# A router's top logit taken tile by tile, and a head's sums moved to GpSimd, in a four-layer graph network on one core

## The chip, the core and the metric

The kernel runs on one NeuronCore of a Trainium2 chip. The core has five engines that run their own instruction streams side by side: TensorE (PE, matrix products into PSUM), VectorE (DVE), ScalarE (ACT), GpSimd (POOL) and SyncE (SP, which here only issues transfers). Each engine takes its instructions in order; semaphores order them against each other. The metric is the device time of one execution in microseconds (us); less is better.

## The reference, cut to what matters

A network of four layers on 1250 nodes with 512 features and 20000 edges. Each layer is a graph step and a feed-forward step, each added to x after a layer norm. The change touches two of the eight steps: the mixture of experts of layer 1 and the first of two attention convolutions of layer 2.

```python
def _L1_ffn_ref(x, Wr, br, W1, b1, W2, b2):        # 8 experts, top 1
    xf = x.reshape(-1, d)
    router_logits = xf @ Wr + br
    topk_logits, topk_idx = jax.lax.top_k(router_logits, 1)
    topk_gates = jax.nn.softmax(topk_logits, axis=1)
    for e in range(8):
        h = relu(xf @ W1[e] + b1[e])
        oe = h @ W2[e] + b2[e]
        out = out + where((topk_idx[:, 0] == e)[:, None], topk_gates * oe, 0.0)

def gat_conv(x, src, dst, W, att_src, att_dst, bias):   # 4 heads of 256
    h = (x @ W).reshape(N, HEADS, HID)
    a_src = sum(h * att_src, axis=-1)
    a_dst = sum(h * att_dst, axis=-1)
    e = leaky_relu(a_src[src] + a_dst[dst], 0.2)
    m = segment_max(e, dst, num_segments=N)
    e = exp(e - m[dst])
    s = segment_sum(e, dst, num_segments=N)
    alpha = e / (s[dst] + 1e-16)
    out = segment_sum(alpha[:, :, None] * h[src], dst, num_segments=N)
    return out.reshape(N, HEADS * HID) + bias
```

With one expert per node the gate is softmax of one number, which is 1; only the index of the largest logit is needed.

## The kernel before

The nodes stand in NT = 10 tiles of P = 125 rows; x stays in SBUF as X. The program is written stage after stage, and a framework schedules the instructions onto the engines, puts in the semaphores and gives out buffers: a tile of a pool or a PSUM bank that one engine writes and another reads brings a wait. It sees dependences by tile, so that two engines that touch different columns of one PSUM tile wait for each other.

**Routing of layer 1.** `l1_route` hands a function `done(i)` to the stage before it (the end of layer 1's graph step, batch normalisation of ten tiles), which calls it as each tile of X is ready. For every pair of tiles, `done` forms the layer norm: statistics on VectorE (`bn_stats`, L2186), a square root on ScalarE (L2193), six small VectorE steps that end in `nmr` (L2194 to L2199), the scaling on ScalarE (`f1n_xn`, L2212), transposes on PE (L2246) and their copy out of PSUM on ScalarE (`f1n_t`, L2253). `later(i, xt)` multiplies the transposed tile with the router's weights (L814): four products that fill 8 columns of one PSUM tile, `f.logits[0]`, which holds the logits of all ten tiles side by side.

`l1_ffn` then sorts the nodes by expert. It adds the bias to all logits at once (L858), takes the maximum and its index for each tile (L863, L864), and makes a mask `mk` of chosen experts (L868). Two products on PE count nodes before each node (L872) and in each tile (L874). From the counts VectorE makes, for each expert, the number of groups of 128 rows (`gn`) and the last group's end (`gend`); from `gend` it derives whether more than 13 groups are in use (`more`) and each group's expert (`eg`, `es`, `ei`, L891 to L899); then each node's place in the sorted order (`inc`, `pos`, `posi`, L900 to L910). Places become one-hot matrices (`sl`, `gr`, L913 to L924), a product turns them into node numbers by group (L927), and `node` (L929) is the list by which GpSimd gathers rows (`fetched`). SP reads `ei` and loads that expert's weights `f1w` and biases `f1b`. PE then transposes the gathered rows (L944) and runs `up` (L953) and `down` for 13 groups.

**First convolution of layer 2.** `gat` is called twice; the first has `kt = 4`, and there `late` is true. It works on weights between all source and destination nodes: a step (h, s) is head h and source tile s, and an array `e` of 125 x 1250. For each step VectorE forms the exponent (`exponents`, L1125), ScalarE takes the exponential (L1126), VectorE multiplies with the number of edges (`counted`, L1131), PE multiplies `e` with the nodes' features into six accumulators (`aggregated`, L1141), and VectorE adds `e` to `sums` (`summed`, L1150), from which the softmax's denominator comes. There are four heads of ten steps. Step n's loop body issues exponents of step n + 2, counts of n + 1, the sum and the products of n. In the first convolution `maxima(2, ...)` for heads 2 and 3 is spread over the first five steps: two maxima of 125 x 1250 (L1068) for each tile, with its mask `g_mb` loaded by GpSimd's queue (L1066). After it `turned(2)` puts their result through PE (L1087). At the end of a head ScalarE copies the accumulators out (`evacuated`, L1155), and in the first step of the next head `rows_out` sums `sums` over its rows on PE (L1164). Tiles `e` come from a pool of seven buffers, so an exponent waits until the readers of the buffer's last tile are done.

Of the kernel before, what the change touches and what calls it, by code (L numbers as in the profile page):

```python
# [9 lines left out]
F32 = mybir.dt.float32  # L10
F16 = mybir.dt.float16
BF16 = mybir.dt.bfloat16
I32 = mybir.dt.int32
U32 = mybir.dt.uint32
U16 = mybir.dt.uint16
AF = mybir.ActivationFunctionType
OP = mybir.AluOpType
AX = mybir.AxisListType
# [5 lines left out]
P = 125  # L24
NT = N // P
# [11 lines left out]
class Net:  # L37
# [760 lines left out]
    def l1_route(self, ctx):  # L798

        nc, a, X, ne = self.nc, self.a, self.X, 8  # L800
        f = self.f1 = SimpleNamespace()
        p = f.p = self.pool(ctx, "f1")
        f.xnd = self.tc.dram_tile([N, D], F32, name="f1xn")
        f.norm = Norm(self, ctx, "f1n", keep="rows", scalar=True)
        f.wr = p.tile([128, 4, ne], F32, name="f1wr")
        nc.gpsimd.dma_start(f.wr, a["L1_ffn_Wr"].rearrange("(k p) e -> p k e", p=128))
        f.br = self.rowbc(p, a["L1_ffn_br"], ne, "f1br")
        f.logits = {}

        def later(i, xt):  # L810
            if not f.logits:
                f.logits[0] = self.bank("f1_ps")
            for k in range(4):
                nc.tensor.matmul(f.logits[0][:P, i * ne:(i + 1) * ne], lhsT=xt[:, k, :],  # L814
                                 rhs=f.wr[:, k, :], start=k == 0, stop=k == 3)

        xts = {}

        def done(i):
            if not f.norm.pair(i, X):  # L820
                return
            for j in (i - 1, i):
                nc.gpsimd.dma_start(f.xnd[j * P:(j + 1) * P, :], f.norm.xn[:, j, :])
                xts[j] = f.norm.turned(j)
            for j in (i - 3, i - 2):
                if j >= 0:
                    later(j, xts.pop(j))
            if i == NT - 1:
                for j in (i - 1, i):
                    later(j, xts.pop(j))  # L830

        return done

    def l1_ffn(self, done):
        nc, tc, a, X = self.nc, self.tc, self.a, self.X
        ne, hid, ng, nm = 8, 256, 17, 13
        ys = tc.dram_tile([ng * 128, D], F32, name="f1ys")
        with ExitStack() as ctx:
            p, xnd = self.f1.p, self.f1.xnd
# [7 lines left out]
            for t in range(NT):  # L847
# [6 lines left out]

            lg = p.tile([P, NT, ne], F32, name="f1lg")
            nc.vector.tensor_tensor(lg, self.f1.logits[0][:P, :NT * ne].rearrange("p (t e) -> p t e", t=NT),  # L858
                                    self.f1.br[:P, None, :].to_broadcast([P, NT, ne]), OP.add)
            m8 = p.tile([P, NT, 8], F32, name="f1m8")  # L860
            i8 = p.tile([P, NT, 8], U32, name="f1i8")
            for i in range(NT):
                nc.vector.max(m8[:, i, :], lg[:, i, :])  # L863
                nc.vector.max_index(i8[:, i, :], m8[:, i, :], lg[:, i, :])  # L864
            i1 = p.tile([P, NT], F32, name="f1i1")
            nc.vector.tensor_copy(i1, i8[:, :, 0])
            mk = p.tile([P, ne, NT], F32, name="f1mk")
            nc.vector.tensor_tensor(mk, i1[:, None, :].to_broadcast([P, ne, NT]),  # L868
                                    self.iota[:P, :ne, None].to_broadcast([P, ne, NT]), OP.is_equal)
# [7 lines left out]
            inc = p.tile([P, ne, NT], F32, name="f1inc")  # L877
# [8 lines left out]
            gn = p.tile([P, ne], F32, name="f1gn")  # L886
            nc.vector.tensor_copy(gn, gi)
            gend = p.tile([P, ne], F32, name="f1gend")
            nc.vector.tensor_tensor_scan(gend, self.ones[:P, :ne], gn, 0.0, OP.mult, OP.add)
            more = p.tile([1, 1], I32, name="f1more")  # L890
            nc.vector.tensor_scalar(more, gend[0:1, ne - 1:], float(nm), -float(nm), OP.max, OP.add)  # L891
            eg = p.tile([1, ng, ne], F32, name="f1eg")
            nc.vector.tensor_tensor(eg, self.iota[0:1, :ng, None].to_broadcast([1, ng, ne]),
                                    gend[0:1, None, :].to_broadcast([1, ng, ne]), OP.is_ge)
            es = p.tile([1, ng], F32, name="f1es")
            nc.vector.tensor_reduce(es, eg, AX.X, OP.add)
            nc.vector.tensor_scalar(es, es, float(ne - 1), None, OP.min)
            ei = p.tile([1, ng], I32, name="f1ei")
            nc.vector.tensor_copy(ei, es)  # L899
            nc.vector.tensor_tensor(gend, gend, gn, OP.subtract)  # L900
            nc.vector.tensor_tensor(inc, inc, tot, OP.subtract)
            nc.vector.scalar_tensor_tensor(inc, gend[:, :, None].to_broadcast([P, ne, NT]), 128.0, inc,
                                           OP.mult, OP.add)
            nc.vector.tensor_tensor(inc.rearrange("p e t -> p (e t)"), inc.rearrange("p e t -> p (e t)"),
                                    ps[:P, :ne * NT], OP.add)
# [2 lines left out]
            nc.vector.tensor_reduce(pos, inc.rearrange("p e t -> p t e"), AX.X, OP.add)  # L908
            posi = p.tile([P, NT], I32, name="f1posi")
            nc.vector.tensor_copy(posi, pos)  # L910

            qi = p.tile([P, 2, NT], I32, name="f1qi")
            nc.vector.tensor_scalar(qi[:, 0], posi, 127, None, OP.bitwise_and)  # L913
# [16 lines left out]
            xg, xt, w, b, h = {}, {}, {}, {}, {}  # L930
# [78 lines left out]
    def gat(self, HT, H, kt, wa, W, bias, name):  # L1009

        nc, tc = self.nc, self.tc
# [5 lines left out]
        with ExitStack() as ctx:  # L1017
            p = self.pool(ctx, name)
# [14 lines left out]
            def wide(rows, what):  # L1033
                return qt.tile([rows, N], F32, name=name + what, tag="t")
# [11 lines left out]
            for h in range(nh):  # L1046
                t = wide(128, "_asb")
# [53 lines left out]
            qb, es, accs, first = {}, {}, {}, {}  # L1101
# [14 lines left out]
            late = kt == 4  # L1116
# [3 lines left out]
            sums = p.tile([P, N], F32, name=name + "_sum")  # L1120
# [25 lines left out]
                    first[h] = e  # L1146

            def summed(h, s):
                if s > 0:
                    nc.vector.tensor_tensor(sums, sums if s > 1 else first.pop(h), es[h, s], OP.add)  # L1150

            def evacuated(h):
                for f in range(2):
# [62 lines left out]
            for n, (h, s) in enumerate(steps):  # L1216
                if late and n < 5:
                    maxima(2, range(2 * n, 2 * n + 2))
                if n == 5:
                    turned(2)  # L1220
                if s == 1 and h + 1 < nh:
                    terms(h + 1)
                if n + 2 < len(steps):
                    exponents(*steps[n + 2])
                if n + 1 < len(steps):
                    counted(*steps[n + 1])
                summed(h, s)
                aggregated(h, s)
                if s == 3 and h > 0:
                    reciprocals(h - 1)  # L1230
                if s == 7 and h > 0:
                    divided(h - 1)
                if s == NT - 1 and h + 1 < nh:
                    evacuated(h)
# [1154 lines left out]
```

## Time and profile before

| What | Value |
|---|---|
| Median of 3 runs | 2718.39 us (2718.12 to 2720.2) |
| The profiled execution | 2713.25 us |
| Its span, first to last instruction | 2711.5 us |
| Mean granted TensorE clock | 0.929 |
| VectorE, exponent L1125, 125x1250 | 1517 ns each, x80 |
| VectorE, count L1131, 125x1250 | 1453 ns each, x80 |
| VectorE, sum L1150, 125x1250 | 1456 ns each, x64 (and 1461 ns, x8) |
| VectorE, maximum L1068, 125x1250 | 1460 ns each, x80 |
| ScalarE, exponential L1126, 125x1250 | 1335 ns each, x80 |
| PE, products L1141 | 519 ns each, x960 |
| PE, logits L814 | 355 ns each, x80 (two records for one product) |

The counts are those of both convolutions together. The profile lists one execution: a busy share for each engine over the span, the chain of work that ended last, groups of instructions by line, and a timeline in which each row is a start, a length, an engine with a line, the operation and its tiles. In brackets stands the idle time of that engine just before, and what ended it. Lengths of rows that follow each other on one engine overlap a little: the end of one lies under the start of the next.

### The profile page before, as it was taken

Reading aid. Unit: us, or ns where it says so; the run is one execution under the profiler, and the core shown is the slowest. Engines: PE = TensorE matmul, PEld = TensorE weight load, DVE = VectorE, ACT = ScalarE, POOL = GpSimd, SP = SyncE. Lnnn points to the kernel's source line nnn. Section 1 sums busy time; section 2 is a strip of 40 time slices with the busy share of each in tenths; the row PEclk is TensorE's granted clock in tenths of the full one; section 3 lists DMA queues with packets and bytes.
Section 4 is the critical chain, followed back from the end, with each engine's and each line's share of the span. In section 5 each row is a group of like instructions: output and inputs, shape, how many; then the busy total and the mean of one; then the engine's idle time right before and its main releaser. Section 6 shows DMA issues by size and latency. Waiting matters only on the chain.

```text
span 2711.5 us, 29770 instructions
## 1 busy us (share of the span) xinstructions
PE 2430.8 (90%) x10367; PEld 1538.4 (57%) x10367; DVE 1415.8 (52%) x3219; ACT 820.3 (30%) x1824; POOL 475.8 (18%) x540
## 2 busy tenths in 40 slices
PE   6899889999996999885879899999999799869996
PEld 3555689999943767764534454445554344445542
DVE  8856562100054888864257995567953653621100
ACT  4541111212123777752122342023421231211110
POOL 0002111211004555511210000100010121122211
PEclk9999769999986999995979999999999899979998
DMA  3112245666605555512832102211122201469996
GB/s 84 51 36 77 70 139 188 213 207 204 199 28 143 149 147 142 143 36 93 333 116 85 60 16 92 83 52 45 44 69 93 86 2 49 155 240 361 365 377 239
DMA packets 106746, 360.03 MB, mean 133 GB/s; under 512 B 34818, under 2 KB 39703, under 8 KB 84828
## 3 DMA queue, kind: packets, MB, share of 16 engines
q1 hardware_dynamic: 59867, 252.68, 26.4%
q0 software_dynamic: 44560, 100.92, 14.1%
q10 hardware_dynamic: 2160, 4.45, 0.5%
q8 instruction: 84, 1.38, 0.2%
q14 instruction: 75, 0.61, 0.1%
HBM read 328.36 MB, written 29.53 MB: 132 GB/s over the span
## 4 chain that ended last, share of the span: by engine, by line
PE 40%; DMA 8%; DVE 6%; issue 2%; ACT 1%; POOL 0%; POOLq 0%; ACTq 0%; SPq 0%; DVEq 0%
PE g_acc L1141 11%; PE g_ps L1097 7%; DMA f3wd<-in_L_ffn_W_down_dram 4%; PE f_ps L1616 3%; PE g_ps L1277 3%; PE f_ps L1590 2%; PE g_ps L1486 2%; PE g_ps L1459 1%; PE g_ps L1464 1%; PE f_ps L1340 1%; DMA f1ys<-f1y 1%; DVE g_junk L1068 1%; PE g_ps L1040 1%; PE ac_ps L1814 1%; DMA CT<-in_L_ffn_W_down_dram 1%
## 5 line engine op out<-in xcount | busy, mean ns | idle before, releaser
L1141 PE MATMUL g_acc<-g_e,g2hh 125*128 125x417 f32 (+1 forms) x960 | 344.6, 519 | 7.4 <-DVE g_e L1131 7.4
L1141 PEld LDWEIGHTS g_acc<-g_e,g2hh 125*128 125x128 f32 x960 | 182.9, 192 | 166.8 <-issue 157.3
L428 POOL DMA_INDIRECT G<-t,SI x160 | 156.4, 978 | 231.7 <-issue 104.2
L1804 ACT ACTIVATE G<-G,ex 128x129 f32<-128x129 f32 x632 | 190.1, 389 | 0.8
L1814 PE MATMUL ac_ps<-G,oh 128*125 128x258 f32 x736 | 187.3, 410 | 1.8 <-DVE g1acc L1823 1.5
L564 PE MATMUL f_ps<-f0xgt,f0w 128*128 128x187 f32 x1024 | 168.8, 325 | 0.1
L1814 PEld LDWEIGHTS ac_ps<-G,oh 128*125 128x125 f32 x736 | 143.5, 200 | 42.3 <-issue 11.9
L575 PE MATMUL f_acc<-f0ht,f0w 128*128 128x187 f32 x1024 | 166.7, 324 | 0.0
L564 PEld LDWEIGHTS f_ps<-f0xgt,f0w 128*128 128x128 f32 x1024 | 165.5, 192 | 0.4 <-DVE f0xgt L105 0.3
L575 PEld LDWEIGHTS f_acc<-f0ht,f0w 128*128 128x128 f32 x1024 | 164.7, 191 | 0.3
L1125 DVE SCALAR_TENSOR_TENSOR g_e<-g_qb,g_a 125x1250 f32<-125x1250 f32 x80 | 120.6, 1517 | 69.3 <-DMA g_qb<-g_qd 61.7
L1126 ACT ACTIVATE g_e<-g_e,g_a 125x1250 f32<-125x1250 f32 x80 | 106.4, 1335 | 137.6 <-DVE g_e L1125 137.3
L1616 PE MATMUL f_ps<-f3wd,f3ht 128*39 128x512 f32 (+1 forms) x544 | 134.6, 613 | 14.2 <-DMA f3wd<-in_L_ffn_W_down_dram 14.1
L1622 DVE TENSOR_SCALAR f3y<-f_ps,f3k_wsel 39x512 f32<-39x512 f32 x32 | 24.0, 749 | 230.7 <-PE f_ps L1616 230.2
L1097 PE MATMUL g_ps<-g22w,g2ht 128*125 128x512 f32 x320 | 138.0, 593 | 0.1
L224 PE MATMUL c_ps<-ohs,ohd 128*125 128x512 f16 (+1 forms) x552 | 108.1, 344 | 22.5 <-DVE ohd L215 13.3
L1068 DVE CUSTOM_DVE_ANT_0 g_junk<-g_mb,g_asb 125x1250 f32<-125x1250 bf16 x80 | 116.8, 1460 | 19.5 <-DMA g_asb<-g_as 15.0
L1131 DVE SCALAR_TENSOR_TENSOR g_e<-g_e,CT 125x1250 f32<-125x1250 f32 x80 | 116.0, 1453 | 7.0 <-ACT g_e L1126 6.7
L1765 DVE TENSOR_REDUCE gm<-mx_ps 125x1 f32<-125x512 f32 x184 | 114.0, 682 | 3.7 <-PE mx_ps L1756 3.7
L592 DVE TENSOR_SCALAR f0y<-f_ps,f0xg,f0r 128x512 f32<-128x512 f32 (+1 forms) x16 | 12.2, 802 | 187.2 <-PE f_ps L590 187.2
L218 DVE TENSOR_SCALAR ohs<-iota,ES 128x1250 f16<-128x1250 f16 x184 | 89.2, 542 | 34.5 <-PE c_ps L224 31.7
L224 PEld LDWEIGHTS <-ohd 128*125 128x125 f16 x552 | 69.0, 137 | 62.3 <-DVE ohd L215 14.0
(678 smaller groups left out, 3862.2 us busy)
## 6 DMA issues: line engine op xcount, KB each, us to landing
f0w<-in_L_ffn_w_dram SPq DMA_DIRECT2D x64, 1024.0 KB
f3wd<-in_L_ffn_W_down_dram SPq DMA_DIRECT2D x48, 1280.0 KB
CT<-in_L_ffn_W_down_dram SPq DMA_DIRECT2D x16, 1280.0 KB
f1w<-in_L_ffn_w_dram SPq DMA_DIRECT2D x13, 1024.0 KB
f3wu<-in_L_ffn_W_up_dram SPq DMA_DIRECT2D x12, 1024.0 KB
g_mb<-mbd POOLq DMA_DIRECT2D x40, 305.2 KB, 3.4
g_qb<-g_qd SPq DMA_DIRECT2D x16, 625.0 KB
f2tv<-in_L_ffn_tv_W_dram SPq DMA_DIRECT2D x16, 512.0 KB
```

The source lines that it names most:

```text
L224: nc.tensor.matmul(pss[i][:P, :cn], lhsT=ohd[g % 2][:, k, :], rhs=ohs[(4 * g + k) % R][:, c0:c0 + cn], start=g == 0 and k == 0, stop=k == ...
L428: self.nc.gpsimd.indirect_dma_start(out=out, out_offset=None, in_=table, in_offset=bass.IndirectOffsetOnAxis(ap=idx, axis=0))
L564: nc.tensor.matmul(ps[:, :cap], lhsT=w[:, k, f * 128:(f + 1) * 128], rhs=xgt[e][:, k, :], start=k == 0, stop=k == 3)
L575: nc.tensor.matmul(acc[e][d][:, :cap], lhsT=w[:, f, d * 128:(d + 1) * 128], rhs=ht[e][:, 4 * c + f, :], start=c == 0 and f == 0, stop=c == ...
L1068: nc.vector.tensor_tensor_reduce(junk, mb, asb[h], 1.0, -3e38, OP.add, OP.max, accum_out=mx[:, i, h:h + 1])
L1097: nc.tensor.matmul(ps[:P, :], lhsT=HT[:, k, i * P:(i + 1) * P], rhs=ws[hf][k // 4][:, k % 4, :], start=k == 0, stop=k == kt - 1)
L1125: nc.vector.scalar_tensor_tensor(e, qb[h][0], A8[:, s, h:h + 1], qb[h][1], OP.add, OP.max)
L1131: nc.vector.scalar_tensor_tensor(e, e, 1.0, self.CT[:, s, :], OP.min, OP.mult)
L1141: nc.tensor.matmul(accs[h][f][c][:, :cn], lhsT=H[:, s, h * 256 + f * 128:h * 256 + (f + 1) * 128], rhs=e[:, c0:c0 + cn], start=s == 0, sto ...
L1616: nc.tensor.matmul(ps[64 * h:64 * h + k, :], lhsT=ht[g][:n, f, j * k:(j + 1) * k], rhs=ws[h][:n, f - f0, :], start=f == 0, stop=f == nf - 1)
L1804: nc.scalar.activation(gv[:, k, h], gv[:, k, h], AF.Copy, scale=ex[:, k, h:h + 1])
L1814: nc.tensor.matmul(ac[j][:P, 0:2 * (ch + 1)], lhsT=v["oh"][:, k, :], rhs=v["G"][:, k, j * 2 * (ch + 1):(j + 1) * 2 * (ch + 1)], start=k == ...
```

## The change

There are three parts.

(a) `later` adds the bias to its tile's eight logits and takes their maximum and index itself, right after the tile's products; `l1_ffn` no longer does so for all tiles.

(b) In `l1_ffn` the steps for `more`, `eg`, `es` and `ei` move behind `posi`. Two copies of one element of `posi` into `more` and `eg` are new; they make these steps depend on `posi`, so that they can't be scheduled before it. The groups' start goes to a tile of its own, `gof`, since `gend` is still needed.

(c) In `summed`, the nine additions of head 0 in the first convolution are issued on GpSimd instead of VectorE.

```diff
         def later(i, xt):
...
             for k in range(4):
                 nc.tensor.matmul(f.logits[0][:P, i * ne:(i + 1) * ne], lhsT=xt[:, k, :],
                                  rhs=f.wr[:, k, :], start=k == 0, stop=k == 3)
+            nc.vector.tensor_tensor(f.lg[:, i, :], f.logits[0][:P, i * ne:(i + 1) * ne], f.br[:P, :], OP.add)
+            nc.vector.max(f.m8[:, i, :], f.lg[:, i, :])
+            nc.vector.max_index(f.i8[:, i, :], f.m8[:, i, :], f.lg[:, i, :])
...
-            lg = p.tile([P, NT, ne], F32, name="f1lg")
-            nc.vector.tensor_tensor(lg, self.f1.logits[0][:P, :NT * ne].rearrange("p (t e) -> p t e", t=NT),
-                                    self.f1.br[:P, None, :].to_broadcast([P, NT, ne]), OP.add)
-            m8 = p.tile([P, NT, 8], F32, name="f1m8")
-            i8 = p.tile([P, NT, 8], U32, name="f1i8")
-            for i in range(NT):
-                nc.vector.max(m8[:, i, :], lg[:, i, :])
-                nc.vector.max_index(i8[:, i, :], m8[:, i, :], lg[:, i, :])
             i1 = p.tile([P, NT], F32, name="f1i1")
-            nc.vector.tensor_copy(i1, i8[:, :, 0])
+            nc.vector.tensor_copy(i1, self.f1.i8[:, :, 0])
...
-            more = p.tile([1, 1], I32, name="f1more")
-            nc.vector.tensor_scalar(more, gend[0:1, ne - 1:], float(nm), -float(nm), OP.max, OP.add)
-            eg = p.tile([1, ng, ne], F32, name="f1eg")
...
-            nc.vector.tensor_copy(ei, es)
-            nc.vector.tensor_tensor(gend, gend, gn, OP.subtract)
+            gof = p.tile([P, ne], F32, name="f1gof")
+            nc.vector.tensor_tensor(gof, gend, gn, OP.subtract)
...
             nc.vector.tensor_copy(posi, pos)
+
+            more = p.tile([1, 1], I32, name="f1more")
+            nc.vector.tensor_copy(more, posi[0:1, 0:1])
+            nc.vector.tensor_scalar(more, gend[0:1, ne - 1:], float(nm), -float(nm), OP.max, OP.add)
+            eg = p.tile([1, ng, ne], F32, name="f1eg")
+            nc.vector.tensor_copy(eg[0:1, 0, 0:1], posi[0:1, 0:1])
+            nc.vector.tensor_tensor(eg, self.iota[0:1, :ng, None].to_broadcast([1, ng, ne]),
+                                    gend[0:1, None, :].to_broadcast([1, ng, ne]), OP.is_ge)
+            es = p.tile([1, ng], F32, name="f1es")
+            nc.vector.tensor_reduce(es, eg, AX.X, OP.add)
+            nc.vector.tensor_scalar(es, es, float(ne - 1), None, OP.min)
+            ei = p.tile([1, ng], I32, name="f1ei")
+            nc.vector.tensor_copy(ei, es)
...
             def summed(h, s):
+
+                eng = nc.gpsimd if late and h == 0 else nc.vector
                 if s > 0:
-                    nc.vector.tensor_tensor(sums, sums if s > 1 else first.pop(h), es[h, s], OP.add)
+                    eng.tensor_tensor(sums, sums if s > 1 else first.pop(h), es[h, s], OP.add)
```

More of the change, by code (lines that the diff above doesn't have):

```diff
@@ L808, in l1_route @@
         f.logits = {}
+        f.lg = p.tile([P, NT, ne], F32, name="f1lg")
+        f.m8 = p.tile([P, NT, 8], F32, name="f1m8")
+        f.i8 = p.tile([P, NT, 8], U32, name="f1i8")
         def later(i, xt):
@@ L889, in l1_ffn @@
             nc.vector.tensor_tensor_scan(gend, self.ones[:P, :ne], gn, 0.0, OP.mult, OP.add)
-            more = p.tile([1, 1], I32, name="f1more")
-            nc.vector.tensor_scalar(more, gend[0:1, ne - 1:], float(nm), -float(nm), OP.max, OP.add)
-            eg = p.tile([1, ng, ne], F32, name="f1eg")
[L893 to L898, printed above, removed]
-            nc.vector.tensor_copy(ei, es)
-            nc.vector.tensor_tensor(gend, gend, gn, OP.subtract)
+            gof = p.tile([P, ne], F32, name="f1gof")
+            nc.vector.tensor_tensor(gof, gend, gn, OP.subtract)
             nc.vector.tensor_tensor(inc, inc, tot, OP.subtract)
-            nc.vector.scalar_tensor_tensor(inc, gend[:, :, None].to_broadcast([P, ne, NT]), 128.0, inc,
+            nc.vector.scalar_tensor_tensor(inc, gof[:, :, None].to_broadcast([P, ne, NT]), 128.0, inc,
                                            OP.mult, OP.add)
```

## The prediction

> **What bounds the kernel now.** I read the page's busy shares first, then the chain of waits, then the timeline of the two places that the diff touches, because a share is a mean over many stages with different limits. The page gives:
>
> ```profile
> PE 2430.8 (90%) x10367; PEld 1538.4 (57%) x10367; DVE 1415.8 (52%) x3219; ACT 820.3 (30%) x1824; POOL 475.8 (18%) x540
> ...
> PE 40%; DMA 8%; DVE 6%; issue 2%; ACT 1%; POOL 0%; POOLq 0%; ACTq 0%; SPq 0%; DVEq 0%
> ```
>
> TensorE (PE) is busy 90% of the span and carries most of the chain; VectorE (DVE) is on it for 6%. An edit on VectorE or GpSimd (POOL) therefore pays only where PE waits, and costs wherever it makes PE wait. So I look at each place.
>
> **Place 1: the routing of layer 1, 1244 to 1280 us.** The timeline of PE, then of VectorE (start, length, line, operation, tiles, count; in brackets the idle time before and what ended it):
>
> ```profile
> 1245.69 6.74 PE L814 MATMUL f_ps<-f1wr,f1n_t 128*125 128x8 f32 x32
> 1252.27 1.91 PE L2246 MATMUL f1n_ps<-ident,f1n_xn 125*128 125x125 f32 x8
> 1254.07 3.53 PE L814 MATMUL f_ps<-f1wr,f1n_t 128*125 128x8 f32 x16
> ...
> 1264.42 3.53 PE L814 MATMUL f_ps<-f1wr,f1n_t 128*125 128x8 f32 x16
> 1271.08 0.71 PE L872 MATMUL f_ps<-f1mk,f1lt 125*125 125x80 f32 x2 [3.13 <-DVE f1mk L868]
> ```
>
> ```profile
> 1248.94 0.16 DVE L2199 SCALAR_TENSOR_TENSOR f1n_nmr<-f1n_mv,f1n_r 125x2 f32<-125x2 f32 x1
> ...
> 1267.98 0.24 DVE L858 TENSOR_TENSOR f1lg<-f_ps,f1br 125x80 f32<-125x80 f32 x1 [7.41 <-PE f_ps L814]
> ...
> 1270.78 0.24 DVE L868 TENSOR_TENSOR f1mk<-f1i,iota 125x80 f32<-125x80 f32 x1
> ```
>
> PE runs without a gap from 1245.69 to 1267.95: logits of tiles 0 to 3 (8 records a tile), transposes of tiles 4 and 5, their logits, and so on. VectorE is idle 7.41 us before L858. After the last logit come one add, ten max and ten index searches: 2.83 us until mk at 1270.78. That tail is what the first part works on.
>
> **Place 2: the first head of layer 2's first convolution, 1463 to 1530 us.** Busy time by stretch (columns: length, then busy us of PE, weight load, VectorE, ScalarE, GpSimd; clock; DMA), and PE's timeline:
>
> ```profile
> 1463.00:1510.00 47.00, 34.69 (x95) 17.61 (x93) 46.83 (x55) 8.74 (x10) 4.23 (x8) 0.86 0.25 74
> 1510.00:1530.00 20.00, 20.00 (x51) 10.14 (x52) 16.67 (x12) 7.43 (x11) 0.00 (x0) 0.90 0.18 64
> ```
>
> ```profile
> 1488.14 11.33 PE L1141 MATMUL g_acc<-g_e,g2hh 125*128 125x417 f32 x24 [3.85 <-DVE g_e L1131]
> 1504.37 2.24 PE L1087 MATMUL g_ps<-ident,g_q 125*4 125x125 f32 x10 [4.89 <-DVE g_q L1076]
> 1509.94 19.09 PE L1141 MATMUL g_acc<-g_e,g2hh 125*128 125x417 f32 x48 [3.33 <-DVE g_e L1131]
> 1528.96 2.41 PE L1164 MATMUL g_ps<-g_sum,ones 125*1 125x417 f32 x6
> ```
>
> Until 1510 VectorE is the bound (46.83 of 47 us busy, PE waits for it three times, 12.1 us); from 1510 PE is. Here nine sums (L1150) lie on VectorE, 1.46 us long and 1.375 apart; six start before 1498, three after 1511. Taking the six away looks like 6 x 1.375 = 8.25 us.
>
> **Part (a), logits tile by tile.** Removed: one add of 125x80 and the searches behind it. Added: ten adds of 125x8 on the same PSUM tile that PE is writing. In the built order of the instructions the first logits matmul of tile j+1 waits for VectorE's add of tile j, since both touch one tile of one bank. And on VectorE's in-order queue the adds of tiles 3, 5 and 7 stand ahead of L2199's nmr of the pairs (4,5), (6,7), (8,9), which ScalarE needs to make what PE transposes next. The two engines so take turns. Walked by hand: a tile's logits take 1.81 us from start to end (3.53 for two, less overlap); matmul to add 0.03 (1267.95 to 1267.98), the add 0.17 (as the 125x8 L881 beside it), VectorE to PE 0.06 (1271.02 to 1271.08).
> Tile 0 ends 1247.50; tile 1 1249.57; tile 2 1251.64; tile 3 1253.71. Its add, then nmr at 1253.95, not 1248.94. ScalarE normalises (0.76), transposes begin 1255.0, not 1252.27. Tiles 4, 5 end 1260.7; add and the rest of the chain, nmr near 1261.8; transposes 1262.7, not 1257.45. Tiles 6, 7 end 1268.4; nmr 1269.0; transposes 1269.9, not 1262.63. Tiles 8, 9 end 1275.6; last add, max, search, cast; mk about 1276.5 instead of 1270.78: **+5.7 us**. The tail does shrink, from 2.83 to 0.9, but 7.6 us come before it. Ends: -1.9 us if PE didn't wait at all (the tail alone); +7 if each exposed turn costs 0.2 more. I take +5.7.
>
> **Part (b), groups' experts behind the places.** L891 to L899 leave the run to posi: they take 0.6 us there (1273.93 to 1274.71, between other steps), but two added copies of 0.14 to 0.17 and the chain's own steps are built between posi and sl (L918, 1.49 us) and just behind it. What follows posi waits as much longer as posi comes earlier: node +0.1. ei comes 3 us later than before against mk, so the loads f1w and f1b, which SP issued 1.1 us behind ei at 1276.13, now issue about with the gather of rows (GpSimd, 1279.64, landed 1286.69). Behind SP's read of ei stand only these loads of the first groups. Cover: the first matmul of the experts (L953, 1288.70) waits for that gather anyway; without cover, since DMA engines are 88% busy from 1277 to 1288, up to +2. I take **+0.3**.
>
> **Part (c), nine sums on GpSimd.** The nearest rows of the operation: L1347 and L1471, two-input adds of 125x512 f32 on GpSimd, 1.26 us; a 128x2 one takes 0.22. So 2.03 ns an element, and 125x1250 is estimated at 0.22 + 1248 x 2.03 = 2.76 us. Lowest end: the one-input cast L312 of 125x1250, 1.25 us.
> Does VectorE run meanwhile? Three rows:
>
> ```profile
> 192.06 2.82 DVE L300 TENSOR_TENSOR C<-S 125x1250 f32<-125x1250 uint16 x2
> ...
> 223.46 2.17 DVE L300 TENSOR_TENSOR C<-S 125x1250 f32<-125x1250 uint16 x1
> ```
>
> ```profile
> 223.07 1.25 POOL L312 CAST CT<-g0ct 125x1250 uint16<-125x1250 f32 x1 [0.29 <-DVE g0ct L105]
> ```
>
> ```profile
> 2172.65 1.27 POOL L1471 TENSOR_TENSOR X<-X,g3bet 125x512 f32<-125x512 f32 x1 [3.41 <-ACT g3n_o L2212]
> ```
>
> ```profile
> 2172.69 1.25 DVE L2199 SCALAR_TENSOR_TENSOR g3n_nmr<-g3n_mv,g3n_r 125x1 f32<-125x1 f32 x1
> ```
>
> L300 alone takes 1.41; begun 0.39 after GpSimd's cast it took 2.17, about the cast's remaining 0.86 more. L2199 on one column normally takes 0.16; begun under a GpSimd add it took 1.25, until the add ended. VectorE stood still. All its large steps here (L1068, L1125, L1131) read two SBUF tensors, like these.
> Here a rule speaks for the change and another against it. The Trainium skill, "Perfetto Trace Analysis", section Optimizing Scalar/DVE Operations: where VectorE is saturated, moving some of its work to GpSimd may make sense, though the same sentence warns of their shared port. By the first half: six sums gone, -8.25, and some 0.7 back, since exponents need the buffer that GpSimd's queue of sums (2.76 each, against an exponent every 4.2) still reads: -7.5. By "SBUF — State Buffer", section SBUF: two separate sides (the first of the two to start holds the shared ports for its whole instruction, the other fully blocks) each sum costs VectorE 2.76 in place of 1.375. The rows decide, and they are of the second kind.
> Sum: six sums before PE's steady run at 1509.94: 6 x (2.76 - 1.375) = +8.3. Sums 7 to 9: VectorE needs 4.19 us a step against PE's 4.22 (42.24 us over ten steps), so 1.385 more each is not covered; two of the three come to stand before steps that PE waits for: +2.6. ScalarE's copies of head 0 out of PSUM (L1155) are built behind one more exponential, +0.8. Together **+11.7**. If the add takes 2.4 us, the same terms give +8.4; at the cast's 1.25, 6 x (1.25 - 1.375) = -0.75. Behind an exponent that waits for a sum's buffer, VectorE's whole queue waits; that is nothing more while blocking has already slowed it by more. GpSimd's own queue: g_mb loads (0.53 each, 3.4 to land) stand behind adds; L1068 uses them two to five VectorE steps (3 to 7 us) later, covered.
>
> **Sum.** +5.7 + 0.1 + 0.3 + 11.7 = +17.8 on the profiled execution's 2713.25 (span 2711.5): 2731. The median of the runs, 2718.39, lies 5.1 above that execution; 2718.4 + 17.8 = **2736**. Later stages begin when these end and PE bounds them, so both delays pass through.
>
> **Rivals.**
> - The other side: GpSimd's adds run beside VectorE in the stretch 1463 to 1510. They take -7.5 from PE's three waits there, which pays the routing's +6.1: 2717, not slower. It decides once a sum costs VectorE less than about 0.3 us in place of 1.375 (6 x 1.1 = 6.6). For: PE waits 12 us for VectorE there. Against: the three rows of blocking, though none is of this size. 0.08.
> - The same, and PE's logits aren't held up either (-1.9): 2718.4 - 7.5 - 1.9 = 2709. Against: the wait is in the built order. 0.06.
> - Blocking smaller than reckoned (the add at 2.0 to 2.4, or VectorE winning turns), +7 to +11, or the routing unharmed with (c) as reckoned, +10: 2725 to 2730. 0.12.
> - More: PE's longer pauses bring more half-clock time (clock 0.86 in the first stretch), or the experts' loads are exposed, +2 to +10 on top: to 2746 and beyond. 0.12.
> - Forecast, 2730 to 2742: 0.62.
> A measurement tells 0.2% (5.4 us) from no change: slower 0.86, same 0.08, faster 0.06. Range 2725 to 2745.
>
> **What would show it.** In place 1, gaps of 0.3 us on PE between tiles with VectorE's add as releaser, larger ones before the transposes; mk near 1276.5. In place 2, GpSimd rows of 2.76 us, VectorE steps under them of 2.8 to 4.2, PE's steady run beginning near 1524 (1509.94 + 5.7 + 0.4 + 8.3). Wrong if VectorE's rows stay at 1.46 under them, or PE's logits stay one block.

## The result, and the profile after

| | before | after |
|---|---|---|
| Median of 7 runs | 2720.2 us (2718.12 to 2726.04) | 2736.05 us (2734.68 to 2744.13) |
| The profiled execution, its span | 2713.25, 2711.5 | 2735.16, 2733.2 |
| GpSimd busy | 475.8 us | 511.0 us |

The kernel is slower: the ratio of the runs is 1.0061, 95% interval 1.0049 to 1.0073, which is 13 to 20 us. The spans of the two profiled executions differ by more, 21.7 us. Set side by side instruction by instruction on PE, they already stand 2.1 us apart at 1229 us, before anything that was changed; 0.9 us come near 1390 and 2.9 us between 2145 and 2175, in stages whose code is the same, and 1.2 us go at the end. So the change is read from its own two stretches. I take each between two fixed instructions of PE: stretch A from the first product of layer 1's batch normalisation (L790 before) to the second count on the mask (L874 before, 42.56 us), and stretch B from the first product of head 0 (L1141 before) to its first row sum (L1164 before, 66.36 us).

**Stretch A, 48.28 us, 5.7 longer.** PE in the changed kernel (here and in all timelines: start, length, engine and line, operation, tiles, count; in brackets idle time and what ended it):

```profile
1247.80 1.69 PE L817 MATMUL f_ps<-f1wr,f1n_t 128*125 128x8 f32 x8
1249.76 1.85 PE L817 MATMUL f_ps<-f1wr,f1n_t 128*125 128x8 f32 x8 [0.26 <-DVE f1lg L819]
1251.95 1.82 PE L817 MATMUL f_ps<-f1wr,f1n_t 128*125 128x8 f32 x8 [0.35 <-DVE f1lg L819]
1254.12 1.81 PE L817 MATMUL f_ps<-f1wr,f1n_t 128*125 128x8 f32 x8 [0.35 <-DVE f1n_s L2201]
1257.11 1.93 PE L2250 MATMUL f1n_ps<-ident,f1n_xn 125*128 125x125 f32 x8 [1.17 <-ACT f1n_xn L2216]
...
1264.66 1.93 PE L2250 MATMUL f1n_ps<-ident,f1n_xn 125*128 125x125 f32 x8 [1.72 <-ACT f1n_xn L2216]
...
1271.86 1.93 PE L2250 MATMUL f1n_ps<-ident,f1n_xn 125*128 125x125 f32 x8 [1.37 <-ACT f1n_xn L2216]
...
1278.91 0.71 PE L870 MATMUL f_ps<-f1mk,f1lt 125*125 125x80 f32 x2 [1.22 <-DVE f1mk L866]
```

What was one unbroken run is now cut at every tile. Between two tiles PE stands 0.26 to 0.35 us for VectorE, and before each pair's transposes 1.2 to 1.7 us for ScalarE. (The row at 1254.12 names a layer norm step, L2201, as releaser; that step follows directly on the tile's add, and the gap is the same.) ScalarE in turn waited for VectorE, whose queue shows why:

```profile
1255.97 0.17 DVE L819 TENSOR_TENSOR f1lg<-f_ps,f1br 125x8 f32<-125x8 f32 x1 [1.19 <-PE f_ps L817]
1256.06 0.15 DVE L2203 SCALAR_TENSOR_TENSOR f1n_nmr<-f1n_mv,f1n_r 125x2 f32<-125x2 f32 x1
```

The add of tile 3 waits for PE, and the layer norm's last step stands behind it. The tail after the last logit has shrunk as meant: 1.22 us of idle PE in place of 3.13. The granted TensorE clock was 0.50 throughout stretch A, in both kernels and in all runs below.

**Stretch B, 76.63 us, 10.3 longer.** GpSimd, then VectorE:

```profile
1467.49 3.91 POOL L1154 TENSOR_TENSOR g_sum<-g_e 125x1250 f32<-125x1250 f32 x1 [0.69 <-DVE g_e L1133]
```

```profile
1467.26 1.45 DVE L1070 CUSTOM_DVE_ANT_0 g_junk<-g_mb,g_asb 125x1250 f32<-125x1250 bf16 x1
1468.63 0.08 DVE L1070 DVE_READ_ACCUMULATOR2_ANT g_mx<- 125x1 f32 x1
1468.63 4.08 DVE L1127 SCALAR_TENSOR_TENSOR g_e<-g_qb,g_a 125x1250 f32<-125x1250 f32 x1
```

The add was issued while VectorE worked on a maximum (1467.26 to 1468.63), and had to wait for it; it ended at 1471.40, so its own work took 2.77 us if it began as the maximum ended. The exponent that VectorE issued at 1468.63 takes 4.08 us where 1.52 is usual. Each sum draws one such row: 4.07, 4.08, 4.08, 4.07 and 3.96 us follow before VectorE is through. The price of a sum is thus 2.5 to 2.6 us of VectorE in place of 1.375. VectorE was busy 75.67 of the stretch's 76.63 us, so that nothing else held it for long. PE pays for it:

```profile
1500.08 10.49 PE L1143 MATMUL g_acc<-g_e,g2hh 125*128 125x417 f32 x24 [6.47 <-DVE g_e L1133]
1522.18 2.28 PE L1089 MATMUL g_ps<-ident,g_q 125*4 125x125 f32 x10 [11.62 <-DVE g_q L1078]
1527.76 14.51 PE L1143 MATMUL g_acc<-g_e,g2hh 125*128 125x417 f32 x36 [3.30 <-DVE g_e L1133]
1542.59 1.67 PE L1143 MATMUL g_acc<-g_e,g2hh 125*128 125x417 f32 x4 [0.32 <-DVE g_e L1133]
1545.78 3.07 PE L1143 MATMUL g_acc<-g_e,g2hh 125*128 125x416 f32 x8 [1.52 <-ACT g2ht L1159]
1548.78 2.41 PE L1168 MATMUL g_ps<-g_sum,ones 125*1 125x417 f32 x6
```

The three waits are 6.5, 11.6 and 3.3 us where they were 3.9, 4.9 and 3.3, and two new ones follow. All of PE's idle time in B is 23.23 us where it was 12.31; its products took no more time than before (53.39 us, before 54.05), at a granted clock of 0.84 where it was 0.87. So the 10.3 us are waits.

### The profile page after: what moved, and what is told of

Same layout as the page of the kernel before. It is cut to its first block, busy times and chain, and to the rows that moved or that the text cites. A ratio compares the mean times of both kernels' runs of the same rounds, so it can differ in the third digit from the quotient of the medians.

```text
span 2733.2 us, 29808 instructions
## 1 busy us (share of the span) xinstructions
PE 2431.8 (89%) x10367; PEld 1537.9 (56%) x10367; DVE 1429.6 (52%) x3221; ACT 820.3 (30%) x1824; POOL 511.0 (19%) x549
## 4 chain that ended last, share of the span: by engine, by line
PE 41%; DMA 7%; DVE 5%; issue 2%; ACT 1%; POOL 0%; POOLq 0%; ACTq 0%; SPq 0%; DVEq 0%
PE g_acc L1143 11%; PE g_ps L1099 7%; DMA f3wd<-in_L_ffn_W_down_dram 4%; PE f_ps L1620 3%; PE g_ps L1281 3%; PE g_ps L1490 2%; PE f_ps L1594 2%; DMA f3wd<-n_L_ffn_W_down_last_dram 2%; PE g_ps L1463 1%; PE g_ps L1468 1%; PE f_ps L1344 1%; PE g_ps L1042 1%; PE f_ps L955 1%; PE f_ps L966 1%; PE ac_ps L1818 1%
## 5 line engine op out<-in xcount | busy, mean ns | idle before, releaser
L1143 PE MATMUL g_acc<-g_e,g2hh 125*128 125x417 f32 (+1 forms) x960 | 343.9, 518 | 11.6 <-DVE g_e L1133 10.1
L1127 DVE SCALAR_TENSOR_TENSOR g_e<-g_qb,g_a 125x1250 f32<-125x1250 f32 x80 | 130.8, 1644 | 69.3 <-DMA g_qb<-g_qd 61.7
L1133 DVE SCALAR_TENSOR_TENSOR g_e<-g_e,CT 125x1250 f32<-125x1250 f32 x80 | 126.5, 1583 | 6.9 <-ACT g_e L1128 6.6
```

Of the source, the lines that this page charges most:

```text
L1127: nc.vector.scalar_tensor_tensor(e, qb[h][0], A8[:, s, h:h + 1], qb[h][1], OP.add, OP.max)
L1133: nc.vector.scalar_tensor_tensor(e, e, 1.0, self.CT[:, s, :], OP.min, OP.mult)
L1143: nc.tensor.matmul(accs[h][f][c][:, :cn], lhsT=H[:, s, h * 256 + f * 128:h * 256 + (f + 1) * 128], rhs=e[:, c0:c0 + cn], start=s == 0, sto ...
```

## The experiments

All times of whole runs scatter more in these sets than in the first (before: 2706 to 2736 us over 93 runs in three sets), so that intervals reach 3 to 5 us to either side. The stretches are much steadier: in the kernels that don't touch them, A is 42.54 to 42.57 us and B 66.1 to 66.8. They decide, each from one profiled execution. Column G is the time from the product that makes the list of nodes to the first gathered group's transposes.

| run | A | G | B | ratio of whole runs, 95% |
|---|---|---|---|---|
| before | 42.56 | 8.12 | 66.36 | |
| after | 48.28 | 8.92 | 76.63 | 1.0061 (1.0049 to 1.0073) |
| e1_sums | 42.55 | 8.02 | 77.29 | 1.0025 (1.0011 to 1.0039) |
| e2_route | 48.26 | 7.90 | 66.72 | 1.0005 (0.9990 to 1.0020) |
| e3_experts | 42.55 | 8.51 | 66.14 | 1.0002 (0.9985 to 1.0019) |
| e4_parity | 46.35 | 7.51 | 66.77 | 0.9996 (0.9980 to 1.0012) |
| e5_eight | 42.26 | 8.42 | 66.58 | 0.9999 (0.9983 to 1.0015) |
| e6_nosums | 42.56 | 7.95 | 59.36 | 0.9966 (0.9949 to 0.9984) |
| e7_memset | 42.57 | 8.39 | 59.23 | 0.9967 (0.9950 to 0.9984) |
| e8_early | 42.55 | 8.64 | 52.82 | 0.9945 (0.9926 to 0.9965) |
| e9_tied | 40.86 | 8.50 | 66.57 | 0.9995 (0.9980 to 1.0011) |
| e10_best | 40.86 | 8.32 | 53.69 | 0.9956 (0.9940 to 0.9973) |
| e11_both | 42.54 | 8.01 | 67.41 | 1.0006 (0.9990 to 1.0022) |

### Each part alone

My theory: the routing costs through turns between PE and VectorE, the sums through GpSimd stopping VectorE. Rival: one of the two does what it is meant to, and the other bears the whole loss.

The kernel before with the sums' edit alone:

```diff
+                eng = nc.gpsimd if late and h == 0 else nc.vector
                 if s > 0:
-                    nc.vector.tensor_tensor(sums, sums if s > 1 else first.pop(h), es[h, s], OP.add)
+                    eng.tensor_tensor(sums, sums if s > 1 else first.pop(h), es[h, s], OP.add)
```

> Part (c) alone: head 0's nine sums on GpSimd, routing as before. Blocking theory: each sum stops VectorE about 2.6 us in place of 1.375; +10.3 us as between the two traces, so 2728 to 2732 beside a before of 2720. Rival, that the sums run beside VectorE and the whole loss is the routing's: -7.5 us.

B grew by 10.9 us, A not at all. The whole runs give +6.8 us (3.0 to 10.6), a little less than that; the median, 2727.32, is just under the range that I named. The rival's -7.5 is out.

The kernel before with the bias, maximum and index moved into `later`, alone:

```diff
+            nc.vector.tensor_tensor(f.lg[:, i, :], f.logits[0][:P, i * ne:(i + 1) * ne], f.br[:P, :], OP.add)
+            nc.vector.max(f.m8[:, i, :], f.lg[:, i, :])
+            nc.vector.max_index(f.i8[:, i, :], f.m8[:, i, :], f.lg[:, i, :])
```

> Part (a) alone: bias, maximum and index after each tile's logits. Theory of the turns between PE and VectorE: +5.7 us, PE's logits in ten rows with gaps, mask near 1276.5 against 1270.8. Rival, that only the tail counts: -1.9 us.

A grew by 5.70 us, the same as in the changed kernel, B stayed. The whole runs, +1.4 us (-2.7 to 5.4), would not have shown a loss by themselves, and 5.7 lies just outside them.

The kernel before with the groups' experts behind `posi`, alone (cut; the steps between are moved as in the change):

```diff
             nc.vector.tensor_copy(posi, pos)
+            more = p.tile([1, 1], I32, name="f1more")
+            nc.vector.tensor_copy(more, posi[0:1, 0:1])
...
+            nc.vector.tensor_copy(ei, es)
```

> Part (b) alone: the groups' experts behind the places. Theory: +0.0 at the list of nodes, up to +0.8 us at the first gathered group because the weight loads are issued later and beside the gather; total within 1 us of before. Rival: the shorter run to the places shows as -0.6 us.

From the counts to the list of nodes it took 7.10 us, before 7.13: the hoped 0.6 us aren't there, since two copies and the moved steps themselves come to stand among the steps behind `posi`. G is 8.51 here, but it lies anywhere from 7.5 to 8.9 in kernels with and without this part, so nothing can be put down to the later loads.

In the stretches the parts add up to the change: 5.7 us in A, and 10.9 in B against 10.3. The whole runs of the parts give only 6.8 + 1.4 + 0.5 = 8.7 us where the change gave 15.9; the intervals, 3 to 5 us to either side for each part, taken together just cover the difference. Whether some of a stretch's loss is made up later in the program isn't shown.

### Routing: the shared tile or the queue?

Two things hold PE up in part (a): the PSUM tile that VectorE reads while PE wants to write it, and the place of the adds on VectorE's queue. With two PSUM tiles in turn PE doesn't wait for the last tile's add (cut; the add, maximum and index are those of part (a), on the tile's own PSUM tile):

```diff
-            if not f.logits:
-                f.logits[0] = self.bank("f1_ps")
+            if not f.logits:
+                f.logits = {c: self.bank("f1_ps") for c in range(2)}
...
-                nc.tensor.matmul(f.logits[0][:P, i * ne:(i + 1) * ne], lhsT=xt[:, k, :],
+                nc.tensor.matmul(f.logits[i % 2][:P, i * ne:(i + 1) * ne], lhsT=xt[:, k, :],
```

> Part (a) with two PSUM tiles, even and odd node tiles in turn, so that PE no longer waits for the add of the tile just before. If the shared PSUM tile were the whole cause, this is -1.9 us against before. If the adds' place on VectorE's queue ahead of the layer norm's last step counts as well, about +3.6 us remain of the +5.7.

A is 46.35: of the 5.7 us, 1.9 went and 3.8 stayed. PE in that run:

```profile
1250.44 6.73 PE L817 MATMUL f_ps<-f1wr,f1n_t 128*125 128x8 f32 x32
1258.90 1.93 PE L2244 MATMUL f1n_ps<-ident,f1n_xn 125*128 125x125 f32 x8 [1.72 <-ACT f1n_xn L2210]
1260.71 3.53 PE L817 MATMUL f_ps<-f1wr,f1n_t 128*125 128x8 f32 x16
1266.35 1.93 PE L2244 MATMUL f1n_ps<-ident,f1n_xn 125*128 125x125 f32 x8 [2.11 <-ACT f1n_xn L2210]
```

The gaps between tiles are gone, the waits for the normalised tiles are not. The smaller part is the shared tile's, the larger the queue's.

If so, a search that stays out of the layer norm's way should gain. Tiles 0 to 7 get a PSUM tile of their own, and are searched in `l1_ffn` as before, but in two goes (cut; `later` now picks the PSUM tile):

```diff
-            for i in range(NT):
-                nc.vector.max(m8[:, i, :], lg[:, i, :])
-                nc.vector.max_index(i8[:, i, :], m8[:, i, :], lg[:, i, :])
+            for c, (t0, t1) in enumerate(((0, 8), (8, 10))):
+                nc.vector.tensor_tensor(lg[:, t0:t1, :],
...
+                for i in range(t0, t1):
+                    nc.vector.max(m8[:, i, :], lg[:, i, :])
+                    nc.vector.max_index(i8[:, i, :], m8[:, i, :], lg[:, i, :])
```

> Search of tiles 0 to 7 from a PSUM tile of their own, behind the layer norm's steps on VectorE and under the logits of tiles 8 and 9 on PE. Theory (only the turns cost, the shorter tail pays): eight searches of 0.21 us and no wait of PE, mask -1.6 us against before, measured from the end of the batch normalisation. Rival, that any search before the last logit delays the layer norm: 0 or later.

A is 42.26, 0.3 shorter instead of 1.6: my expectation missed. VectorE, then PE in that run:

```profile
1267.04 0.22 DVE L862 TENSOR_TENSOR f1lg<-f_ps,f1br 125x64 f32<-125x64 f32 x1 [2.43 <-PE f_ps L815]
1267.18 0.15 DVE L2202 SCALAR_TENSOR_TENSOR f1n_nmr<-f1n_mv,f1n_r 125x2 f32<-125x2 f32 x1
```

```profile
1268.23 1.93 PE L2249 MATMUL f1n_ps<-ident,f1n_xn 125*128 125x125 f32 x8 [1.23 <-ACT f1n_xn L2215]
```

The schedule put one step of the layer norm, the last, behind the new add. It waited through the 2.43 us with the add, PE stood 1.23 us before the last transposes, and the gain was nearly spent. So the same two rows, now with one add instead of ten. One line ties the add behind that step:

```diff
+            nc.vector.tensor_copy(lg[:, 0, 0:1], self.f1.norm.nmr[:, NT - 1:NT])
             for c, (t0, t1) in enumerate(((0, 8), (8, 10))):
```

> As the run with eight tiles searched early, but a copy of one element of the layer norm's last result into the logits' tile ties the early search behind it, so that no layer norm step stands behind an add that waits for PE. If the order on VectorE's queue is what cost the earlier version its gain: mask -1.4 to -1.6 us against before, PE's logits and transposes without a gap. If the search itself disturbs PE: -0.3 us again.

A is 40.86, 1.7 us shorter than before, slightly more than expected, and PE has no gap until the mask:

```profile
1251.12 3.53 PE L815 MATMUL f_ps<-f1wr,f1n_t 128*125 128x8 f32 x16
1254.50 1.91 PE L2250 MATMUL f1n_ps<-ident,f1n_xn 125*128 125x125 f32 x8
1256.30 3.53 PE L815 MATMUL f_ps<-f1wr,f1n_t 128*125 128x8 f32 x16
1261.28 0.68 PE L876 MATMUL f_ps<-f1mk,f1lt 125*125 125x80 f32 x2 [1.45 <-DVE f1mk L872]
```

That shows the cause by its removal. Of a whole run it is too little to be seen (-1.4 us, -5.4 to 3.0).

### The sums: what stops VectorE?

First what there was to gain. Head 0's sums are left out, and one fill by ones stands in their place:

```diff
-                if s > 0:
+                if late and h == 0:
+                    if s == 1:
+                        first.pop(h)
+                        nc.vector.memset(sums, 1.0)
+                elif s > 0:
```

> Head 0's nine sums left out, with one fill of the sums by ones in their place, so the denominators of that head aren't computed. What the sums cost on VectorE before: first row sum on PE -7 us (six sums of 1.375 less the fill). If VectorE were not the bound there, 0.

B shortens by 7.0 us, as named, but not by the sum that I gave: the fill ran on VectorE at 1353 us, long before the stretch, so it takes nothing off the 8.25. VectorE is the bound there, and 7 us was about the most that moving the sums away could bring. Of the 7.0, 4.1 are PE's waits; for the other 2.9 PE's products took less time (51.11 us, before 54.05), at a granted clock of 0.91 in place of 0.87.

Then GpSimd is kept as busy, but without reading. In the place of each sum but the first it copies one column and fills the tile twice (cut; the rest is as in the last run):

```diff
+                    elif s > 1:
+                        nc.gpsimd.tensor_copy(sums[:, s:s + 1], es[h, s][:, 0:1])
+                        nc.gpsimd.memset(sums, 1.0)
+                        nc.gpsimd.memset(sums, 1.0)
```

> As without the sums, but GpSimd copies one column of each weight tile and then fills 125x1250 of ones twice, which reads nothing from SBUF (the denominators of that head aren't computed). If GpSimd's reads of SBUF are what stops VectorE, VectorE's rows under the fills stay near 1.46 us, and the row sum comes near -7 us, or some later for GpSimd's queue. If any large GpSimd instruction stops it, rows of VectorE under the fills are longer by the fill's length, and the row sum comes 5 us or more after before's.

B is 59.23, as without the sums. GpSimd and VectorE in the same 4 us:

```profile
1470.67 1.26 POOL L1154 COPY g_sum<-g_e 125x1 f32<-125x1 f32 x1 [0.70 <-DVE g_e L1131]
1471.99 1.14 POOL L1155 MEMSET g_sum<- 125x1250 f32 x1
1473.19 1.14 POOL L1156 MEMSET g_sum<- 125x1250 f32 x1
1474.40 0.29 POOL L1154 COPY g_sum<-g_e 125x1 f32<-125x1 f32 x1
```

```profile
1470.43 1.46 DVE L1068 CUSTOM_DVE_ANT_0 g_junk<-g_mb,g_asb 125x1250 f32<-125x1250 bf16 x1
1471.81 0.09 DVE L1068 DVE_READ_ACCUMULATOR2_ANT g_mx<- 125x1 f32 x1
1471.81 1.47 DVE L1131 SCALAR_TENSOR_TENSOR g_e<-g_e,CT 125x1250 f32<-125x1250 f32 x1
1473.18 1.46 DVE L1068 CUSTOM_DVE_ANT_0 g_junk<-g_mb,g_asb 125x1250 f32<-125x1250 bf16 x1
1474.56 0.09 DVE L1068 DVE_READ_ACCUMULATOR2_ANT g_mx<- 125x1 f32 x1
```

Under two fills VectorE keeps its 1.46 us. The copy of a single column, which reads, takes 1.26 us when it comes 1.14 before VectorE goes on to its next step (at 1471.81), and 0.29 when it comes 0.16 before (at 1474.56): both times it ends some 0.12 us behind that point, so it waits for VectorE's step to end. The fills write as much as the sums do. So it is the reading of SBUF by GpSimd that excludes VectorE's two-input steps, and, by the stretched rows of the changed kernel, the other way round. This is what the Trainium skill, "SBUF — State Buffer", section SBUF: two separate sides, says of an operation with two SBUF inputs, with its limit that it holds only against a GpSimd operation that reads SBUF.

Does it hurt only because VectorE is full? VectorE's timeline of the kernel before, just ahead of stretch B:

```profile
1431.63 0.17 DVE L1076 SCALAR_TENSOR_TENSOR g_q<-g_ac,g_mx 125x20 f32<-125x20 f32 x1
1447.69 2.95 DVE L1125 SCALAR_TENSOR_TENSOR g_e<-g_qb,g_a 125x1250 f32<-125x1250 f32 x2 [15.88 <-DMA g_qb<-g_qd]
```

It idles 15.88 us, waiting for the rows of the first pair of heads, and then does twenty maxima of the second pair, most of them inside the stretch that it bounds. Ten of them are moved ahead, into the idle time:

```diff
             late = kt == 4
-            if not late:
-                maxima(2)
+            maxima(2, range(5 if late else NT))
...
-                    maxima(2, range(2 * n, 2 * n + 2))
+                    maxima(2, range(5 + n, 6 + n))
```

> Sums on VectorE as before; five of the ten tiles of the second pair's maxima moved ahead, into the 15.9 us in which VectorE waits for the rows of the first pair. Ten maxima of 1.375 us leave the stretch that VectorE bounds: first row sum -12 to -14.6 us, PE's waits of 3.9, 4.9 and 3.3 us nearly gone. Rival, that buffers or the mask loads hold the moved maxima back: -3 us or less.

B is 52.82, 13.5 us shorter, and the whole kernel is faster: 0.9945 (0.9926 to 0.9965). Eight of the ten ran in VectorE's idle time, which has gone to 4.62 us, and PE's waits have gone to 1.8, 2.5 and 0.3:

```profile
1458.23 1.52 DVE L1124 SCALAR_TENSOR_TENSOR g_e<-g_qb,g_a 125x1250 f32<-125x1250 f32 x1 [4.62 <-DMA g_qb<-g_qd]
```

```profile
1490.38 4.47 PE L1140 MATMUL g_acc<-g_e,g2hh 125*128 125x417 f32 x12 [1.82 <-DVE g_e L1130]
1497.31 3.77 PE L1140 MATMUL g_acc<-g_e,g2hh 125*128 125x417 f32 x10 [2.46 <-DVE g_e L1130]
```

The waits are not the whole gain. Stretch B before and in this run (length, busy us of PE, weight load, VectorE, ScalarE, GpSimd; granted clock; DMA):

```profile
1462.60:1528.96 66.36, 54.05 (x144) 27.74 (x143) 63.90 (x66) 16.22 (x19) 4.23 (x8) 0.87 0.23 72
1471.58:1524.40 52.82, 48.21 (x144) 25.25 (x142) 52.74 (x51) 17.83 (x20) 2.12 (x4) 1.00 0.21 64
```

PE's idle time fell from 12.31 to 4.61 us, which is 7.7 of the 13.5. The other 5.8 are PE's own: the same products took 48.21 us in place of 54.05, with a granted clock of 1.00 in place of 0.87. I had no such term; what raised the clock wasn't tested.

The sums go to GpSimd again, on top of the moved maxima:

```diff
+                eng = nc.gpsimd if late and h == 0 else nc.vector
                 if s > 0:
...
+                    eng.tensor_tensor(sums, sums if s > 1 else first.pop(h), es[h, s], OP.add)
```

> The maxima moved ahead and head 0's sums on GpSimd. VectorE then has some room in the first steps. If blocking costs VectorE its time wherever it is nearly full: first row sum +10 us or more after that of the kernel with the maxima alone, thus -3 to 0 against before. If the sums only hurt because VectorE was overfull: no later than with the maxima alone, -13.5.

B is 67.41: 14.6 us longer than with the maxima moved alone, and 1.0 longer than before, just past the end of what I expected. PE waited 9.9 us more, and its products took 4.7 us more, at a granted clock of 0.92 in place of 1.00. So the loss didn't go away, but the question isn't answered: with the maxima moved VectorE was still busy 52.74 of B's 52.82 us, and had no room. What a sum on GpSimd costs where VectorE has idle time isn't shown.

Last, the moved maxima with the tied search, sums on VectorE:

> The tied early search and the maxima moved ahead, together. The two lie in different stages, so they add: -1.5 at the mask and -13.5 at the first row sum, -15 us in all, some 0.9945 or less of before.

A is 40.86 and B 53.69, together 14.4 us less; the whole runs give 0.9956 (0.9940 to 0.9973), 7 to 16 us less. That is short of the 0.9945 that I named, which lies inside the interval. B is 0.9 longer than with the maxima alone, though PE waits less (3.56 us): its products took 50.13 us at a granted clock of 0.97. This version is faster than the kernel before, and so than the changed one. Whether the search adds anything to the moved maxima alone can't be told from the whole runs; in its stretch it does.

## Why the prediction was right

It named 2736 us; 2736.05 was measured. That close a hit is luck: 17.8 us were added to 2718.39, the median then known, while in the measured set the kernel before stands at 2720.2, so that the change is 15.9 us (13 to 20). By its steps (measured: the difference of the two profiled executions within the stretch):

| step | predicted | measured |
|---|---|---|
| (a) mask | +5.7 | +5.7 |
| (b) list of nodes | +0.1 | 0.0 |
| (b) first gathered group | +0.3 | +0.8, within the scatter of G |
| (c) until PE's steady run | +8.3 | +8.3 |
| (c) from there to the row sum | +3.4 | +2.0 |
| sum | +17.8 | +16.8 |

- **The walk of part (a) held step by step.** With the 2.12 us taken off that this execution was late before the stretch, transposes begin at 1254.99, 1262.54 and 1269.74 us, where 1255.0, 1262.7 and 1269.9 were named, and the mask at 1276.49 for 1276.5. What made it work was to read the order on VectorE's queue, and not only who waits for whom: e4_parity puts two thirds of the loss there.
- **Part (c): the add's length was right** (2.76 reckoned from the 512-wide rows, 2.77 measured), and so was the exclusion; of the two passages of the skill, the warning of the shared port held (it stands in the sentence behind the advice, not in the same one). The GpSimd rows are 3.91 us long and not 2.76, as the sign was named, since they hold the wait for VectorE. The rival in which the adds run beside VectorE put the gain at 7.5; e6_nosums shows 7.0 for it, so its size was fair and only its condition fails.
- **The +8.3 came out right partly by two errors that cancel.** A sum cost VectorE 1.2 us more than before, not 1.385: the six stretched rows are 15.4 us over their usual lengths in all, less 8.25 for the sums that left. The rest, 8.3 - 7.2, is in good part maxima that now stand next to each other. Two that follow directly start 1.50 us apart, and 1.375 when another step lies between; two such pairs in B before are eight after, some 0.75 us.
- **The term that was mis-sized is the tail.** I let two of the sums 7 to 9 hold PE for 1.3 us each, and ScalarE's copies for 0.8. PE stood 0.32 for VectorE and 1.52 for the copies (the rows at 1542.59 and 1545.78): the first was too large and the second too small, 1.8 in all for 3.4. The lower end for an add of 2.4 us was also reckoned wrong: the same terms give about +8.9, not +8.4.
- **PE's longer pauses brought no loss through the clock here.** I had given that a chance, on the high side. The granted clock in B did fall, from 0.87 to 0.84, but PE's products took no longer; in A it was 0.50 before and after.
- **The step from the profiled execution to the median was needed.** The execution of before was 5 to 7 us under its kernel's median, and the two executions differ by 5 us in stages that nobody changed. A prediction made against the span and compared with another span would have seemed 4 us too low.

## What to carry to other kernels

- A small step moved early onto an in-order queue costs by its place, not by its length. A 0.17 us add that waits for PE delays all that stands behind it; ask what that is, and tie the step behind the chain that feeds the engine it waits for.
- Here work moved from VectorE to GpSimd took no time off VectorE, since both read SBUF: a sum of 1.4 us on one became 2.6 us of standstill on it. Look first for idle time on the engine that is full: using 11 of the 16 idle microseconds just ahead of the stretch made it 13.5 shorter.
- When a stretch changes its length, take apart the bound engine's waits and its own time, and read the granted clock beside them: of those 13.5 us, 5.8 were PE's own time.
- Read local edits from a stretch between two instructions of the bound engine. These repeat here to within 0.03 us (A) and 0.7 us (B), while whole runs of one kernel scatter over 20.

## What the runs showed of the hardware beyond that

- The length of a GpSimd row includes its wait for VectorE: the page gives 3922 ns as the mean of eight of the sums, some 2.77 us of it work. A sum in e11_both that hardly had to wait took 2.83 us in all.
- A GpSimd fill of 125x1250 f32 takes 1.14 us and doesn't disturb VectorE, though a copy of one column next to it is held more than 1 us by VectorE.
